# Where eight steps of a dense product stand between five rounds of graph sums

## The chip, the cores and the metric

The kernel runs on one core of one Trainium2 chip. The metric is the device time of one execution in microseconds (us). The core has five engines that run their own queues: TensorE (PE; its weight loads are shown as PEld), VectorE (DVE), ScalarE (ACT), GpSimd (POOL) and SyncE (SP, which here only issues DMAs). Semaphores order them.

## The reference

A pre-norm residual block around a two-layer graph attention network, on 3125 nodes with 768 features and 53125 edges (25000 in each direction and a loop for each node), sorted by destination. A second loop for each node is added inside (in the sum as "2 x"). Layer 1 has 4 heads of 256, layer 2 one head of 768.

```python
def gat_conv(x, edge_index, W, a_src, a_dst, bias, heads, out_ch, concat):
    ...
    xl = (x @ W).reshape(n, heads, out_ch)
    e = leaky_relu(alpha_src[src] + alpha_dst[dst], 0.2)
    m = segment_max(e, dst); e = exp(e - m[dst])
    s = segment_sum(e, dst)
    out = segment_sum(xl[src] * (e / (s[dst] + 1e-16))[:, :, None], dst)
    return out + bias
...
h0 = relu(layernorm(x))
h1 = relu(layer_norm(gat_conv(h0, ..., W1, ...), g1, be1)) + (h0 @ Wr1 + br1)
h  = layer_norm(gat_conv(h1, ..., W2, ...), g2, be2) + (h1 @ Wr2 + br2)
return x + h
```

What matters below is the last but one line: for each node, layer 2 needs a weighted sum over the gathered rows of its neighbours (the graph part), a softmax for its weights, and the dense product h1 @ Wr2 (the residual part).

## The kernel before

The nodes are split into 25 tiles (NB) of 128, the last with 53. First the norm and layer 1 run, then the dense product of layer 2, which writes a table in DRAM: for each node 768 features, its source score and padding, 784 float32. Then follows the loop over the node tiles of layer 2 (from L1232), in which alone the change lies.

*The gathers.* The edges of a tile fill at most 17 slots (J) of 128 edges. `fetch` (L1336) issues one indirect DMA on POOL's queue for each slot (`gather`, L206 to L214): 128 rows of the table into one of 36 buffers (RING). A gather waits until the sums have read what stood in its buffer; so POOL runs two tiles ahead of the sums and no further.

*The sums.* `summed` (L1399) does a tile in five rounds of three or four slots, ROUNDS = (0,5,9,13), (1,6,10,14), (4,11,15), (2,8,16), (3,7,12). They are called r0 to r4 here. A round is 12 to 16 matmuls (L1419): weights are a 128x32 block of the attention weights w, four column quarters of PE run at once, and the 768 features go in two halves of 384 into the PSUM buffer pa. After each round `fetch` asks for as many further slots as the round set free.

*The residual steps.* `residuals` (L1300) is a generator. For each tile it computes h1 @ Wr2 over NK2 = 8 chunks of the contraction; each step, s0 to s7, is one chunk: two dense products (L190), which are four matmuls of 128x384 in the trace. All eight add into one PSUM buffer pr, of which there is one only. s1 also asks SP for the h1 of the tile after next (`load_h1`, L1274), s3 asks SP for the rows of x of the next tile (`load_xr`, L227), and s7 is followed by two sums on DVE (L1315 adds the biases in pr; L1316 adds pr to the rows of x), after which pr is free. `filled(n)` (L1326) runs the next n steps. Three tiles' steps (AHEAD) are run ahead of the loop, so tile b runs the steps of tile b + 3, and the last three tiles have none.

*The softmax of the next tile.* After r2 of tile b, PE transposes the scores of tile b + 1 (L1376, five times 128x128; they were copied from the gathered rows by ACT, L1358), DVE adds the mask and finds the maximum (L1380 to L1385), ACT takes the exponential (L1384, L1387, L1388) and prepares the mask after that (L1363, L1364). After r4, PE transposes the exponentials back (L1392), and DVE and ACT copy them to w (L1395, L1396).

*The end of a tile.* `finish` starts behind r4 (L1432, adds the tile's own rows) and goes on in r0 and r1 of the next tile: L1434, the norm (L514 to L524), L1437, L1438 and the store.

The queues of PE, ACT and DVE run in the order in which the program is written (`tc.manual_schedule`, L1463); those of SP and POOL are ordered by the planner. The list STEPS (L1235) says how many steps `filled` runs behind each round, at the end of the round's turn (L1514). With STEPS = [0, 1, 1, 2, 4] a tile's order on PE is

r0, r1, s0, r2, L1376, s1, r3, s2, s3, r4, L1392, s4, s5, s6, s7.

Of the kernel before, what the change touches and what calls it, by code (L numbers as in the profile page):

```python
# [43 lines left out]
@with_exitstack  # L44
def preln_gat2_kernel(
    ctx: ExitStack,
    tc: tile.TileContext,
    x, src, dst,
    W1, a_src1, a_dst1, b1, g1, be1, Wr1, br1,
    W2, a_src2, a_dst2, b2, g2, be2, Wr2, br2,  # L50
    out,
):

    pool = ctx.enter_context(tc.tile_pool(name="flag", bufs=1))
    flag = pool.tile([1, 1], I32, name="flag")  # L60
    in_order(tc, x, src, dst, W1, a_src1, a_dst1, b1, g1, be1, Wr1, br1,
             W2, a_src2, a_dst2, b2, g2, be2, Wr2, br2, out, flag)
    other = tc.nc.values_load(flag[0:1, 0:1], min_val=0, max_val=1)
    with tc.If(other > 0):
        any_order(tc, x, src, dst, W1, a_src1, a_dst1, b1, g1, be1, Wr1, br1,
                  W2, a_src2, a_dst2, b2, g2, be2, Wr2, br2, out)
# [3 lines left out]
def in_order(  # L70
# [1161 lines left out]
    with tc.tile_pool(name="m2", bufs=1, reuse_waits="tile") as mp, \  # L1232
            tc.tile_pool(name="pg2", bufs=1, space=PSUM, reuse_waits="tile") as pp:
        AHEAD = 3
        STEPS = [0, 1, 1, 2, 4]  # L1235
        RING = 36
        f = C2 // 2

# [87 lines left out]
        def filled(n):  # L1326
            for _ in range(n):
                next(fill, None)
# [128 lines left out]
        def own_share(b):  # L1457
            r = rows_of(b)
            own, v = owns[b][:r], shares[b][1][:r]
            nc.gpsimd.tensor_scalar(own, own, v[:, 2:3], v[:, 3:4], op0=OP.mult, op1=OP.mult)  # L1460
            nc.gpsimd.tensor_tensor(own, own, b2_b[:r], OP.add)

        with tc.manual_schedule(engines={PE, ACT, DVE}):  # L1463
# [16 lines left out]
            for b in range(NB):  # L1480
# [3 lines left out]
                for k in range(len(ROUNDS)):  # L1484
# [23 lines left out]
                    if b + 1 < NB and k == (1 if last else 4):  # L1508
# [3 lines left out]
                        if last:  # L1512
                            own_share(b + 1)
                    filled(STEPS[k])  # L1514
                if b + 2 < NB:
# [476 lines left out]
```

## Time and profile before

| | us |
|---|---|
| median of three runs | 1879.6 |
| their range | 1866.58 to 1886.49 |
| the profiled execution | 1891.63 |
| its span in the trace | 1889.8 |

The span has four stages: up to 1120 the norm and layer 1, to 1264.8 the dense product of layer 2, to 1821.3 the loop over tiles with residual steps, to 1889.8 the last tiles, which have none. By stage (span and its length, then the busy time and number of instructions of PE, PEld, DVE, ACT and POOL, then the clock that PE was granted as a share of full speed, the busy share of the DMA engines and GB/s):

```profile
0.00:1120.00 1120.00, 1083.61 (x7871) 665.12 (x7872) 697.43 (x1963) 224.91 (x604) 445.08 (x463) 0.99 0.78 285
1120.00:1264.80 144.80, 116.61 (x721) 61.57 (x721) 60.36 (x178) 27.12 (x72) 73.13 (x80) 0.95 0.85 316
1821.30:1889.80 68.50, 41.89 (x371) 16.22 (x370) 37.65 (x71) 19.62 (x59) 22.85 (x23) 0.81 0.52 174
```

In the rows of the trace "L190 MATMUL pr<-wr,h" is a group of instructions of line 190 with the tile that is written, the tiles that are read, the shapes and, behind the x, how many there are. A figure in brackets is the idle time of the engine just ahead and what released it; "issue" means that the trace shows nothing for which the engine waited. In a table of waits the columns are the engine and its line, what it waited for, the us in total, how often, and the longest. PE's matmuls overlap, so a group's length is from its first start to its last end.

### The profile page before, as it was taken

Reading aid. Unit: us, or ns where it says so; the run is one execution under the profiler, and the core shown is the slowest. Engines: PE = TensorE matmul, PEld = TensorE weight load, DVE = VectorE, ACT = ScalarE, POOL = GpSimd, SP = SyncE. Lnnn points to the kernel's source line nnn. Section 1 sums busy time; section 2 is a strip of 40 time slices with the busy share of each in tenths; the row PEclk is TensorE's granted clock in tenths of the full one; section 3 lists DMA queues with packets and bytes.
Section 4 is the critical chain, followed back from the end, with each engine's and each line's share of the span. In section 5 each row is a group of like instructions: output and inputs, shape, how many; then the busy total and the mean of one; then the engine's idle time right before and its main releaser. Section 6 shows DMA issues by size and latency. Waiting matters only on the chain.

```text
span 1889.8 us, 31224 instructions
## 1 busy us (share of the span) xinstructions
PE 1718.8 (91%) x11522; PEld 955.7 (51%) x11522; DVE 1006.8 (53%) x2604; ACT 450.9 (24%) x1312; POOL 867.9 (46%) x908
## 2 busy tenths in 40 slices
PE   8999999999899999999999999958888888898885
PEld 5666665666465565555555544423333333343332
DVE  7683436988735665565565566313344343334336
ACT  2222331001211222122122111213333233323332
POOL 2000112000456666666666666255656556555562
PEclk9999999999999999999999999978998998989887
DMA  7833548331799999999999999588989999899883
GB/s 234 291 101 128 139 116 313 125 129 58 263 375 389 374 397 378 405 371 404 345 397 379 360 393 353 205 332 292 318 300 320 326 314 314 293 309 326 303 282 121
DMA packets 172393, 546.67 MB, mean 289 GB/s; under 512 B 30259, under 2 KB 55625, under 8 KB 172104
## 3 DMA queue, kind: packets, MB, share of 16 engines
q0 software_dynamic: 99632, 386.94, 56.5%
q1 hardware_dynamic: 68206, 147.26, 22.6%
q10 hardware_dynamic: 4394, 10.39, 1.4%
q8 instruction: 94, 1.54, 0.3%
q14 instruction: 67, 0.55, 0.1%
HBM read 492.19 MB, written 65.62 MB: 295 GB/s over the span
## 4 chain that ended last, share of the span: by engine, by line
PE 75%; issue 11%; DVE 7%; another core or an unknown queue 2%; DMA 2%; ACT 2%; POOL 0%; SPq 0%; ACTq 0%; DVEq 0%; POOLq 0%
PE pr L190 16%; PE pm L190 11%; PE p L190 11%; PE pa L775 10%; PE pa L1419 10%; PE pm L1027 7%; PE pq L580 3%; PE mix L1392 1%; PE p L1190 1%; DMA w<-in_L_gnn_W_dram 1%; PE mix L1376 1%; DMA g<-table,idx_s 1%; DVE w L752 1%; PE pt L859 1%
## 5 line engine op out<-in xcount | busy, mean ns | idle before, releaser
L210 POOL DMA_INDIRECT g<-table,idx_s x393 | 377.4, 960 | 470.9 <-PE pq L610 167.9
L214 POOL DMA_INDIRECT g<-table,hi_s x423 | 431.5, 1020 | 233.7 <-issue 96.0
L1419 PE MATMUL pa<-g,w 128*32 128x384 f32 x1956 | 230.0, 529 | 77.5 <-issue 63.9
L190 PE MATMUL pr<-wr,h 128*128 128x384 f32 x768 | 285.9, 520 | 3.9 <-issue 3.9
L775 PE MATMUL pa<-g,w 128*32 128x256 f32 x3912 | 261.2, 387 | 14.2 <-issue 7.7
L190 PE MATMUL p<-w,h1T 128*128 128x384 f32 (+1 forms) x768 | 267.7, 496 | 0.2
L190 PEld LDWEIGHTS pr<-wr,h 128*128 128x128 f32 x768 | 150.2, 205 | 121.8 <-issue 50.9
L775 PEld LDWEIGHTS pa<-g,w 128*32 128x32 f32 x3912 | 124.9, 110 | 142.6 <-issue 56.7
L190 PEld LDWEIGHTS p<-w,h1T 128*128 128x128 f32 x768 | 139.8, 189 | 113.2 <-issue 22.2
L1419 PEld LDWEIGHTS pa<-g,w 128*32 128x32 f32 x1956 | 63.4, 114 | 217.1 <-issue 201.9
L752 DVE TENSOR_TENSOR w<-oh,al 128x128 f32<-128x128 f32 (+1 forms) x416 | 131.8, 317 | 60.3 <-PE pa L775 13.9
L190 PE MATMUL pr<-h0k,wr 128*128 128x256 f32 (+1 forms) x576 | 143.9, 393 | 3.6 <-issue 3.1
L1027 PE MATMUL pm<-h0g,wr 128*128 128x512 f32 x288 | 131.9, 605 | 0.0
L190 PE MATMUL pm<-w,h0g 128*128 128x344 f32 x432 | 130.7, 457 | 0.3 <-ACT h0g L861 0.3
L190 PE MATMUL pm<-w,h0l 128*128 128x344 f32 x432 | 129.5, 454 | 0.0
L190 PEld LDWEIGHTS pr<-h0k,wr 128*128 128x128 f32 x576 | 106.0, 191 | 35.9 <-issue 17.0
L751 DVE TENSOR_SCALAR oh<-iota_f,rel_s 128x32 f32<-128x32 f32 (+1 forms) x416 | 113.5, 273 | 1.2 <-issue 0.9
L958 POOL DMA_DIRECT2D hot_d<-ohd x25 | 13.4, 534 | 212.6 <-DVE own L531 128.0
L190 PEld LDWEIGHTS pm<-w,h0g 128*128 128x128 f32 x432 | 81.1, 192 | 39.7 <-issue 0.9
L190 PEld LDWEIGHTS pm<-w,h0l 128*128 128x128 f32 x432 | 80.5, 190 | 39.1 <-issue 0.2
L520 ACT ACTIVATE bn_sd<-bn_mv,eps 128x1 f32<-128x1 f32 (+1 forms) x50 | 14.7, 295 | 353.2 <-DVE bn_mv L516 314.6
L1315 DVE TENSOR_TENSOR pr<-pr,ball_b 128x768 f32<-128x768 f32 x24 | 23.2, 967 | 132.5 <-PE pr L190 62.6
(295 smaller groups left out, 1748.3 us busy)
## 6 DMA issues: line engine op xcount, KB each, us to landing
s<-slo_d SPq DMA_DIRECT2D x25, 544.0 KB
table<-row SPq DMA_DIRECT2D x24, 512.0 KB
own<-table SPq DMA_DIRECT2D x24, 512.0 KB
h1T_d<-h1T SPq DMA_DIRECT2D x24, 512.0 KB
h<-h1T_d SPq DMA_DIRECT2D x22, 512.0 KB
table<-row SPq DMA_DIRECT2D x24, 392.0 KB
ring<-in_x_dram SPq DMA_DIRECT2D x24, 384.0 KB
xr<-in_x_dram SPq DMA_DIRECT2D x24, 384.0 KB
```

The lines of the kernel that those rows point to most:

```text
L190: nc.tensor.matmul(out_, lhsT, rhs, start=start, stop=stop)
L210: nc.gpsimd.indirect_dma_start(out=g, out_offset=None, in_=table[:, :], in_offset=bass.IndirectOffsetOnAxis(ap=idx_s[:, c], axis=0))
L214: nc.gpsimd.indirect_dma_start(out=g, out_offset=None, in_=table[:, :], in_offset=bass.IndirectOffsetOnAxis(ap=idx_k[:, c], axis=0), bound ...
L580: nc.tensor.matmul(q[:, j], oh[:P, o:o + 128], tabs[:, i], start=(i == 0), stop=(i == 2))
L751: nc.vector.tensor_scalar(oh, iota_f[:, lo:hi], rel_s[:, c:c + 1], None, op0=OP.is_equal)
L752: nc.vector.tensor_tensor(w, oh[:, None, :].to_broadcast([128, heads, hi - lo]), al[:, POS[j], :, b:b + 1].to_broadcast([128, heads, hi - ...
L775: nc.tensor.matmul(pa[p0:p0 + 32, o // f, o % f:o % f + n], w[:, o // cols, :], g[:, o:o + n], start=to not in opened, stop=False, skip_gr ...
L859: nc.tensor.transpose(pt[:, k, :r], xt[:, (k0 + k) * 128:(k0 + k + 1) * 128], ident[:r, :r])
L1027: nc.tensor.matmul(pm, wr1[:, k, m * 128:(m + 1) * 128], groups[gi][:, k, :], start=(k == 0), stop=(k == NK1 - 1))
L1190: nc.tensor.transpose(pt[:, k, :r], z[:, (k0 + k) * 128:(k0 + k + 1) * 128], ident[:r, :r])
L1315: nc.vector.tensor_add(pm[:, :, :f], pm[:, :, :f], halves(ball_b))
L1419: nc.tensor.matmul(pa[p0:p0 + 32, i, :f], w_, g[:, i * f:(i + 1) * f], start=(i, q) not in opened, stop=False, skip_group_check=True)
```

## The change

The list of steps behind the five rounds is changed, and nothing else:

```diff
@@ -1232,7 +1232,7 @@
         AHEAD = 3
-        STEPS = [0, 1, 1, 2, 4]
+        STEPS = [1, 1, 1, 1, 4]
         RING = 36
```

The order on PE becomes

r0, s0, r1, s1, r2, L1376, s2, r3, s3, r4, L1392, s4, s5, s6, s7.

s0 now stands between r0 and r1, s1 between r1 and r2, and s2 ahead of r3 with nothing but s3 behind r3. s1's request for h1 moves with it. s3 to s7, their requests and the two sums on DVE stand where they stood.

## The prediction

> **What bounds the kernel now.** I read the busy times by stage first, to see what the changed loop is worth, then the PE timeline of one whole node tile, then POOL's, DVE's and ACT's timelines of the same tile, and last the sums of waits in the loop.
>
> ```profile
> span 1889.8 us, 31224 instructions
> core 0: us, PE busy (x) PEld busy (x) DVE busy (x) ACT busy (x) POOL busy (x), PEclk, DMA share, GB/s
> 1264.80:1821.30 556.50, 476.65 (x2564) 212.79 (x2565) 211.36 (x392) 179.26 (x577) 326.88 (x343) 0.90 0.90 306
> ```
>
> The changed list is used only between 1264.8 and 1821.3 us. PE is busy for 476.65 of 556.5 us there; DVE, ACT and POOL for less than 60% each. In front of and behind this stretch nothing is edited. One tile of it, as PE saw it (start, us, what ran, idle before it):
>
> ```profile
> 1522.88 5.33 PE L190 MATMUL pr<-wr,h 128*128 128x384 f32 x16
> 1528.13 2.79 PE L1419 MATMUL pa<-g,w 128*32 128x384 f32 x32
> 1530.85 1.56 PE L190 MATMUL pr<-wr,h 128*128 128x384 f32 x4
> 1532.34 1.50 PE L1419 MATMUL pa<-g,w 128*32 128x384 f32 x16
> 1533.77 0.77 PE L1376 MATMUL mix<-ident,slots 128*128 128x128 f32 x5
> 1534.37 1.46 PE L190 MATMUL pr<-wr,h 128*128 128x384 f32 x4
> 1535.76 1.50 PE L1419 MATMUL pa<-g,w 128*32 128x384 f32 x16
> 1537.18 2.85 PE L190 MATMUL pr<-wr,h 128*128 128x384 f32 x8
> 1539.96 1.17 PE L1419 MATMUL pa<-g,w 128*32 128x384 f32 x8
> 1541.74 0.48 PE L1419 MATMUL pa<-g,w 128*32 128x384 f32 x1 [0.61 <-issue]
> 1542.47 0.50 PE L1419 MATMUL pa<-g,w 128*32 128x384 f32 x1 [0.25 <-issue]
> 1544.59 0.48 PE L1419 MATMUL pa<-g,w 128*32 128x384 f32 x1 [1.62 <-issue]
> 1545.99 0.95 PE L1419 MATMUL pa<-g,w 128*32 128x384 f32 x5 [0.92 <-issue]
> 1546.87 1.33 PE L1392 MATMUL mix<-ident,e 128*128 128x128 f32 x5
> 1547.99 6.34 PE L190 MATMUL pr<-wr,h 128*128 128x384 f32 x16
> ```
>
> From s4 of one tile to s4 of the next (1522.88 to 1547.99) it is 25.1 us. L1419 are the sums: r0 and r1 run together (32 matmuls from 1528.13), then come step s0 of the residual (L190, 4 matmuls), r2, the score transposes L1376, s1, r3, s2 and s3, r4, the transposes of the exponentials L1392, and s4 to s7. PE runs without a pause up to the middle of r4. There, from 1541.13 (1539.96 + 1.17) to 1545.99, it does three matmuls, and the idle time has no releaser but "issue". What ends this hole stands in POOL's timeline, the gathers for a later tile:
>
> ```profile
> 1517.49 0.95 POOL L210 DMA_INDIRECT g<-table,idx_s  x1 [0.30 <-issue]
> 1519.75 2.20 PE L1419 MATMUL pa<-g,w 128*32 128x384 f32 x5 [0.93 <-issue]
> 1530.36 0.95 POOL L210 DMA_INDIRECT g<-table,idx_s  x1 [3.17 <-PE pa L1419]
> 1535.38 0.95 POOL L210 DMA_INDIRECT g<-table,idx_s  x1 [0.30 <-issue]
> 1540.38 0.95 POOL L210 DMA_INDIRECT g<-table,idx_s  x1 [0.30 <-issue]
> 1542.88 1.00 POOL L214 DMA_INDIRECT g<-table,hi_s  x1 [0.30 <-issue]
> 1546.77 0.94 POOL L210 DMA_INDIRECT g<-table,idx_s  x1 [2.88 <-PE pa L1419]
> 1539.01 0.83 DVE L1380 CUSTOM_DVE_ANT_0 mix<-mix,pen 128x640 f32<-128x640 f32 x1 [6.57 <-remote]
> ```
>
> POOL starts at 1530.36, some 0.8 us after r0's last sum, and issues 11 gathers back to back, one per 1.25 us, until 1543.88. The first four take buffers freed by r0, the next four (from 1535.38) by r1, the last three (from 1540.38) by r2. PE resumes 2.1 us after that run's end; in the tile before, the run ended at 1518.44 and PE resumed 1.3 us later, at 1519.75. While the run lasts, PE's results reach the others late: L1376 ends at 1534.54 by PE's record, but L1380, which needs only that, starts at 1539.01, 4.5 us later. So I read this loop as a cycle: r0 done, POOL's run, 2 us, the rest of r4, L1392, s4 to s7, next r0. PE's own work between r0 and r4 has slack against it.
>
> [...]
>
> **The change part by part.** s0, s1 and s2 each move one round earlier; s3 to s7 stay, with the load of xr that s3 issues and the two DVE sums of s7. Eight steps a tile remain, so PE's total work is the same. The new order is r0 s0 r1 s1 r2 L1376 s2 r3 s3 r4 L1392 s4 to s7, in 22 tiles (25 less the three whose successors' residuals are done ahead).
>
> ```profile
> 1528.24 0.97 DVE L1315 TENSOR_TENSOR pr<-pr,ball_b 128x768 f32<-128x768 f32 x1 [3.96 <-issue]
> 1529.24 0.96 DVE L1316 TENSOR_TENSOR xr<-pr,xr 128x768 f32<-128x768 f32 x1
> 1541.95 0.83 ACT L1387 ACTIVATE e<-e,top 128x640 f32<-128x640 f32 x1
> 1528.23 0.32 SPq L1274 DMA_DIRECT2D h<-h1T_d  x1
> 1543.56 0.33 SPq L227 DMA_DIRECT2D xr<-in_x_dram  x1
> ```
>
> *s0 gets a wait.* It writes the one buffer pr, which L1316 still reads until 1530.20 (1529.24 + 0.96). r0 takes half of 2.79 us and ends at 1529.5. So s0 waits 0.7 us; until now r1's 1.4 us covered that. Everything on PE's queue behind s0 waits with it.
>
> *r1 and r2 finish later.* r1 stands behind the wait and s0's 1.5 us: it ends at about 1533.1, not 1530.9 (+2.2). r2 stands behind s1 as well: 1536.0, not 1533.8 (+2.2). r1's buffers are wanted by POOL at 1535.38 (slack 2.3 left), r2's at 1540.38 (4.4 left by the records).
>
> *The softmax of the next tile starts later.* L1376 ends 2.2 later; with the same lateness L1380 starts at 1541.2, and the exponential L1387, which ends 3.8 us behind L1380's start (1542.78), ends at 1545.0. L1392 takes it at 1546.87, so 4.1 us of cover shrink to 1.9. If it is gone, each further us is one on the path.
>
> *r3 and r4.* r3 ends 2.2 us later, at 1539.5, and POOL wants its buffers at 1546.77. r4 starts only the 0.7 us of s0's wait later, as the same four steps stand ahead of it in both.
>
> *Queues.* s1's load of h1 sits on SP and waits for the previous residual's end anyway (issued at 1528.23, just behind s7's end); s1 itself comes 1.2 us earlier but reads another buffer, loaded a tile before. The xr load (1543.56) stays behind s3. POOL's instructions keep their order. DVE's only edit is that L1380 and the normalization behind it in its queue begin later; L1432 at 1546.98 had 3.44 us of idle before it, so it covers this:
>
> ```profile
> 1546.98 1.02 DVE L1432 SCALAR_TENSOR_TENSOR pa<-own,v,pa 128x768 f32<-128x768 f32 x1 [3.44 <-PE pa L1419]
> PE pa L1419 <- issue: 63.3, 62, 5.9
> ```
>
> *The sum.* What counts is how much of r4 is left when the hole ends. Low end: nothing is lost, because the hole ends with POOL's run, and POOL's run starts with r0, which is not moved: 0. High end: if PE stops after the same number of results, counted from the run's start, then two dense groups (s0 and s1, 8 matmuls) and r1's 16 stand where before r1, s0 and r2 (36) stood, 12 fewer matmuls; 12 sums at 0.09 us (1.50 / 16) are 1.1 us. The 0.7 us of the wait alone would be 0.7. A gain below nothing is the second rival's. Neither end is nearer to a row, since no row shows which matmul PE is held at by count; I take the middle, +0.6 us a tile, times 22: **+13 us**. The profiled execution took 1891.6 us, so it would become 1905. That execution stands 0.6% above the median of the runs shown (1879.6), so on the median I forecast 1879.6 + 13 = **1893 us**.
>
> **The rivals.** *First, slower: r2's results hold up POOL.* The last three gathers need r2's result by about 1539.6 (1540.38 less the 0.8 that r0's took). By the records r2 ends at 1536.0, so this decides once results are more than 3.6 us late; L1376, right behind r2, was 4.5 late. It would cost 0.9 us (4.5 - 3.6) and, if the four extra dense results of s1 come out at the pace of the hole (three matmuls in 4.9 us at the worst; 0.5 us each, my estimate, if L1376's 4.5 us are shared out over its five transposes and r2's last four results), 2 us more: 0.9 to 2.9, say 1.5 us x 22 = +33, 1913 us. For it: the 4.5 us. Against: that is the lateness of L1376, not of r2's own results, which came earlier.
>
> *Second, faster: the run is cut in two.* If POOL has to stop after eight gathers, at about 1540.1, PE's results would come 2.1 us later, at 1542.2, instead of 1546. r4 could end near 1543.5, and L1392 would wait for the exponential: L1380 at 1542.2 plus 3.8 gives 1546.0, 0.9 us sooner than 1546.87. With a shorter hole s4 to s7 run in 5.33 us instead of 6.34, another 1.0:
>
> ```profile
> 1683.29 6.96 PE L190 MATMUL pr<-wr,h 128*128 128x384 f32 x16
> POOL g L210 <- PE pa L1419: 114.1, 39, 8.6
> ```
>
> The same 16 matmuls took 5.33, 6.34 and 6.96 us in three tiles, so up to 1.6 us lie there. Half of the 1.9 us in 22 tiles is -20, all of it -42: 1860 to 1838, and 1860 is what I give it. For it: waits of POOL for sums are cheap now (39 waits, 114.1 us, and the ends of runs are where PE recovers). Against: it needs the very event of the first rival, and then that the later gathers are not missed.
>
> [...]
>
> *Third, nothing happens.* The low end of the sum: POOL's run sets the cycle and all else fits beneath it: 1880 us.
>
> **How the numbers follow.** About 1% (19 us) is what a measurement of this kernel can tell from no change. Forecast (+0 to +1.1 us a tile, 1880 to 1904, middle 1893): chance 0.40; as the top of it and the softmax's thin cover reach over 1%, I put 0.27 of it within 1% and 0.13 slower. First rival 0.22: 0.17 slower, 0.05 within. Second rival 0.23: 0.21 faster, 0.02 within. Third 0.15, all within. Together: faster 0.21, within 1% 0.49, slower 0.30. The range leaves out half of the second rival's chance (below 1860) and the far end of the first's (above 1925, more than 2 us a tile): 1860 to 1925. The forecast's own range is 1880 to 1904.
>
> **What would show it.** Step by step, in a typical tile of the changed kernel: about 0.7 us of PE idle before the first L190 group, released by L1316; r1 and r2 2 us later behind r0; POOL still with a run of 11 gathers 1.25 us apart, first one 0.8 us behind r0 (a run of 8 with a pause in it speaks for a rival, and whether r4 then ends sooner or later says which); the hole in r4 still ending 1.3 to 2.1 us behind that run, with more sums behind it; L1380 about 2 us later, its exponential still ahead of L1392; s4 to s7 still at 5.3 to 7.0 us. The forecast is wrong if L1392 starts to wait for ACT, if POOL pauses within its run, or if the hole is gone.

## The result, and the profile after

| | before | changed |
|---|---|---|
| median, us | 1883.05 (4 runs) | 1939.41 (4 runs) |
| range, us | 1866.58 to 1892.15 | 1928.9 to 1951.44 |
| profiled execution's span, us | 1889.8 | 1927.1 |

The ratio is 1.0306, with a 95% interval of 1.0254 to 1.0358. The changed kernel is slower by 3%, 56 us; the forecast was +13, and the time lies above its range.

First the same stretch of both traces, from the score transposes L1376 of the second tile to those of the twenty-second, 20 tiles (columns as in the table by stage above). Before:

```profile
1273.00:1802.20 529.20, 451.81 (x2444) 202.42 (x2440) 204.67 (x377) 169.49 (x539) 310.66 (x327) 0.91 0.90 309
```

After:

```profile
1274.60:1837.20 562.60, 470.23 (x2441) 197.37 (x2442) 203.44 (x377) 169.49 (x539) 308.41 (x324) 0.92 0.86 289
```

A tile went from 26.5 to 28.1 us (529.2 and 562.6 over 20), which gives 33 of the 37 us between the two spans. (The medians are 56 us apart: the changed kernel's traced execution is the fastest of its four, and that of the kernel before is slower than its median.) The engines run nearly the same number of instructions; the DMA engines are less busy (0.86 after 0.90). So something waits longer. One tile of the changed kernel on PE, with the start of the softmax on DVE in its place by time:

```profile
1535.00 1.50 PE L1419 MATMUL pa<-g,w 128*32 128x384 f32 x16
1537.16 1.53 PE L190 MATMUL pr<-wr,h 128*128 128x384 f32 x4 [0.67 <-PE pa L1419]
1538.62 1.50 PE L1419 MATMUL pa<-g,w 128*32 128x384 f32 x16
...
1541.54 1.50 PE L1419 MATMUL pa<-g,w 128*32 128x384 f32 x16
1542.96 0.77 PE L1376 MATMUL mix<-ident,slots 128*128 128x128 f32 x5
...
1544.95 1.50 PE L1419 MATMUL pa<-g,w 128*32 128x384 f32 x16
...
1547.87 0.83 PE L1419 MATMUL pa<-g,w 128*32 128x384 f32 x2
1549.21 1.18 PE L1419 MATMUL pa<-g,w 128*32 128x384 f32 x3 [0.50 <-issue]
1551.45 0.83 DVE L1380 CUSTOM_DVE_ANT_0 mix<-mix,pen 128x640 f32<-128x640 f32 x1 [12.15 <-remote]
...
1556.98 1.56 PE L1419 MATMUL pa<-g,w 128*32 128x384 f32 x6 [1.62 <-issue]
1558.47 1.33 PE L1392 MATMUL mix<-ident,e 128*128 128x128 f32 x5
1559.60 6.78 PE L190 MATMUL pr<-wr,h 128*128 128x384 f32 x16
```

PE is stopped in r4 as before, but from 1548.7 to 1557.0, 8.3 us in place of 4.9. It does eight matmuls in that time (three in the shown tile of the kernel before), and no single pause is longer than 1.62 us. POOL in the same tile:

```profile
1537.22 0.95 POOL L210 DMA_INDIRECT g<-table,idx_s  x1 [7.66 <-issue]
...
1547.29 0.95 POOL L210 DMA_INDIRECT g<-table,idx_s  x1 [0.30 <-PE pa L1419]
...
1553.56 1.00 POOL L214 DMA_INDIRECT g<-table,hi_s  x1 [0.30 <-issue]
1557.84 0.95 POOL L210 DMA_INDIRECT g<-table,idx_s  x1 [3.27 <-remote]
1559.09 0.95 POOL L210 DMA_INDIRECT g<-table,idx_s  x1 [0.30 <-issue]
1568.53 0.94 POOL L210 DMA_INDIRECT g<-table,idx_s  x1 [8.48 <-issue]
```

The run behind r0 lasts from 1537.22 to 1554.56: 14 gathers 1.25 us apart, where there were 11. PE resumes 2.4 us after its end. The short run behind r4 has 2 gathers in place of 5; then POOL stands idle for 8.5 us until the next r0 is done. Three gathers have moved from the short run into the long one.

The other tiles of the same trace show that r4 grows with the run. From its first start to its last end r4 takes 5.8 to 6.1 us in the tiles with a run of 11 gathers, 7.9 with 12, 9.3 with 13 and 10.6 to 10.7 with 14. (Three of the 20 tiles had broken runs; they took 5.8, 5.2 and 1.5 us. Undisturbed, r4's 16 matmuls take 1.50.)

The three gathers moved in POOL's queue. In the two built programs POOL's instructions are the same, but at 13 tile ends their order differs. Written by the round that sets the gather's buffer free (n0 is the next tile's r0):

```
before   r3 r3 r4 r4 r4 | n0 n0 n0 n0 r1 r1 r1 r1 r2 r2 r2
changed  r3 r3 | n0 r4 r4 r4 n0 n0 n0 r1 r1 r1 r1 r2 r2 r2
```

What stands behind the bar waits until the next tile's r0 is done. The first n0 is the buffer of slot 16. At two of three tile ends the last slot of one tile and the first of the next are one gathered block, so its buffer is free only after the next tile's r0. `fetch` asks for buffers in ring order, so that gather comes ahead of r4's three in the program text. POOL's queue is arranged by the planner; in the kernel before it put r4's three gathers first, in the changed one it does so ever less: 1 of them stands behind n0 at three tile ends, 2 at two and all 3 at eight. The trace bears this out with runs of 12, 13 and 14 gathers at these ends. Why the planner arranged it so is not shown. That is 31 gathers more than before; times 1.25 us 39 us, against 37.3 between the two spans. That these agree so closely is luck, as the medians are 56 us apart.

### The profile page after: what moved, and what is told of

The parts are those of the page before. It is cut to its first block, busy times and chain, and to the rows that moved or that the text cites. A ratio compares the mean times of both kernels' runs of the same rounds, so it can differ in the third digit from the quotient of the medians.

```text
span 1927.1 us, 31193 instructions
## 1 busy us (share of the span) xinstructions
PE 1741.0 (90%) x11522; PEld 951.2 (49%) x11522; DVE 1005.8 (52%) x2604; ACT 451.1 (23%) x1312; POOL 870.4 (45%) x908
## 4 chain that ended last, share of the span: by engine, by line
PE 80%; issue 11%; DVE 4%; another core or an unknown queue 2%; ACT 2%; DMA 1%; SPq 0%; DVEq 0%; ACTq 0%
PE pr L190 17%; PE pm L190 13%; PE p L190 13%; PE pa L775 12%; PE pa L1419 10%; PE pm L1027 7%; PE pq L580 3%; PE p L1190 1%; PE mix L1392 1%; PE pt L859 1%; PE mix L1376 1%; DMA g<-table,hi_s 1%; DVE bn_st L514 0%; DVE xr L1316 0%
## 5 line engine op out<-in xcount | busy, mean ns | idle before, releaser
L1419 PE MATMUL pa<-g,w 128*32 128x384 f32 x1956 | 252.8, 517 | 82.1 <-issue 76.5
L1380 DVE CUSTOM_DVE_ANT_0 mix<-mix,pen 128x640 f32<-128x640 f32 x25 | 20.8, 833 | 259.1 <-remote 251.7
```

The costliest lines, as they stand in the source:

```text
L1380: nc.vector.tensor_tensor_reduce(out=sums_, in0=sums_, in1=pen, scale=1.0, scalar=-BIG, op0=OP.add, op1=OP.max, accum_out=top)
L1419: nc.tensor.matmul(pa[p0:p0 + 32, i, :f], w_, g[:, i * f:(i + 1) * f], start=(i, q) not in opened, stop=False, skip_group_check=True)
```

## The experiments

Theory Q: the time comes from POOL's queue. Theory S: it comes from the moved steps themselves, by s0's wait and the later results of r1 and r2. All times are medians in us; in each comparison the kernels ran beside the kernel before on the same chip. Brackets give the ratio to the kernel before and its 95% interval.

**The changed steps with the queue of before.** `fetch` asks for every buffer that is free, so r4's three come first, and POOL's queue is written out by hand:

```diff
-            while asked < len(slots_due) and asked < min(unused, default=0) + RING:
-                b, j = slots_due[asked]
-                i = asked % RING
+            for a, (b, j) in enumerate(slots_due):
+                if a in asked or (a >= RING and a - RING in unused):
+                    continue
+                i = a % RING
...
-        with tc.manual_schedule(engines={PE, ACT, DVE}):
+        with tc.manual_schedule(engines={PE, ACT, DVE, POOL}):
```

> The changed steps (1, 1, 1, 1, 4), but POOL's queue written out by hand in the order it had before: the three gathers into the buffers of r4 stand ahead of the one that waits for the next tile's r0. Theory Q (the time comes from POOL's queue, where 31 gathers of 1.25 us slid behind a gather that waits for r0, 39 us): within 15 us of the kernel before, about 1885, runs of 11 gathers behind r0. Theory S (the time comes from the steps themselves: s0's wait of 0.7 us and late results of r1 and r2): stays near the changed kernel, 1930 to 1945.

**The old steps with the program's order.** The second half of that diff alone, with `fetch` as it was, so n0 stands first at each of the 14 tile ends that share a block:

> The steps of before (0, 1, 1, 2, 4), but POOL's queue in program order, so that at each of 14 tile ends the gather that waits for the next r0 stands ahead of r4's three. Theory Q: 14 or so times 3 times 1.25 us, some +50 us or more, 1930 to 1945, runs of 14 gathers behind r0 where before there were 11. Theory S: no change, 1875 to 1890.

**The control.** Both halves of the diff, and the old steps:

> The control: the steps of before and POOL's queue written out by hand in the order it had before. Both theories: as before, 1875 to 1890. If the hand-written queue itself costs or gains something, it shows here.

Measured in one comparison, before 1886.98: changed steps with the old queue 1888.62 (ratio 1.0025, 0.9990 to 1.0060); old steps with the program's order 1941.50 (1.0305, 1.0228 to 1.0383); control 1883.90 (0.9978, 0.9941 to 1.0014). One tile of the changed steps with the old queue, the first and the last gather of its run:

```profile
1526.57 0.95 POOL L210 DMA_INDIRECT g<-table,idx_s  x1 [3.90 <-PE pa L1419]
...
1539.10 1.01 POOL L214 DMA_INDIRECT g<-table,hi_s  x1 [0.30 <-issue]
```

and one of the old steps with the program's order, with the end of its r4:

```profile
1547.98 0.95 POOL L210 DMA_INDIRECT g<-table,idx_s  x1 [8.33 <-issue]
...
1564.36 1.01 POOL L214 DMA_INDIRECT g<-table,hi_s  x1 [0.30 <-issue]
1567.06 1.54 PE L1419 MATMUL pa<-g,w 128*32 128x384 f32 x2 [0.61 <-issue]
```

The first run has 11 gathers, the second 14, and 14 stand at each of the 14 shared tile ends of that trace. r4 takes a median of 10.1 us over 20 tiles there, 5.8 with the queue put back, 6.4 in the control and 6.6 in the kernel before.

With the queue put back the loss is gone, and with the queue spoilt and no step moved the loss is there. Q holds and S falls: the steps alone cost 4.7 us (1888.62 less 1883.90). That is not clear of noise: the ten runs of each overlap (1880.9 to 1899.74 and 1874.19 to 1892.78). The queue written by hand is not quite the one of before: by the traces no gather of r4 stands behind n0 in it, where in the kernel before 4 do (1 early in the loop, 3 at its last tile). The two programs that give the 4.7 us share it.

**A queue with a break.** If PE is held as long as POOL's run lasts, the run behind r0 should be cut. On top of the control, r2's three gathers are asked for after r3, behind one that needs r3:

```diff
-        def fetch():
+        def fetch(k=None):
...
+            if k == 2:
+                return
+            due = [a for a in range(len(slots_due)) if a not in asked and (a < RING or a - RING not in unused)]
+            if k == 3 and len(due) > 3:
+                due.insert(0, due.pop(3))
...
```

> The steps of before, and POOL's run behind r0 cut in two: behind the eight gathers of r0 and r1 stands one that waits for r3, ahead of r2's three. If PE is held in r4 because its results come out late as long as POOL's run lasts (theory Q's base), POOL stops after 8 gathers, PE's results come about 2 us later, r4 ends before POOL's second run does, and a tile gets 1 to 3 us shorter: 1815 to 1865, with the hole in r4 gone or under 2.5 us. If the hole has another cause, POOL's later gathers only come later: 1880 to 1920.

Measured in the same comparison: 1856.51 (0.9851, 0.9776 to 0.9925), so faster than the kernel before by 0.7 to 2.2%, and 27 us below the control. In that trace PE around r4 (its lines stand 4 further down, so L1423 are the sums and L1396 is L1392):

```profile
1549.56 2.85 PE L190 MATMUL pr<-wr,h 128*128 128x384 f32 x8
1552.34 1.50 PE L1423 MATMUL pa<-g,w 128*32 128x384 f32 x16
1553.77 0.77 PE L1396 MATMUL mix<-ident,e 128*128 128x128 f32 x5
1554.37 5.33 PE L190 MATMUL pr<-wr,h 128*128 128x384 f32 x16
```

r4 runs through without a hole, and s4 to s7 take 5.33 us. Of 20 tiles r4 takes its undisturbed 1.50 us in 15, and 2.7 at most. But the hold has partly moved: in the tile shown, r2 was held instead, from 1536.7 to 1541.4, where POOL's short run had grown into the long one. Over the 20 tiles PE's pauses with releaser "issue" sum to 20.6 us ahead of the sums, after 45.6 in the control, but to 31.5 ahead of the other groups, after 10.1; together they hardly shrank. PE's busy time did, from 449.29 to 430.93 us, at a granted clock of 0.96 after 0.92. So it is shown that the break wins time and that r4's hole goes with the run, not that PE is held less in all.

**One part of the change at a time.** Steps [1, 0, 1, 2, 4] move s0 alone; [0, 2, 1, 1, 4] move s1 and s2 and leave s0. The built programs show 4 gathers behind n0 for the first, as before, and 41 for the second; 35 for the changed kernel. With them went the changed steps with the break:

> Steps 1, 0, 1, 2, 4: of the change only s0's move ahead of r1, so its wait of 0.7 us for pr is there in 22 tiles; s1 and s2 stand as before, and POOL's queue keeps the order of before. Theory Q: the queue is what costs, so no more than the wait's 15 us, most of it hidden in the hole of r4: 1880 to 1900. Theory S (s0's wait and what it delays is the price): well over 1900, half or more of the +57.

> Steps 0, 2, 1, 1, 4: s0 stays behind r1 and so has no wait for pr; s1 and s2 are a round earlier, r1 ends as early as before. In this program's queue on POOL 41 gathers stand behind one that waits for the next r0, where the kernel before has 4 and the changed one 35. Theory Q: 37 more times 1.25 us = +46, 1925 to 1945. Theory S: no wait of s0 and no later r1, so at most r2's delay, 1880 to 1895.

> The changed steps with the hand-written queue on POOL that has a break behind eight gathers. Theory Q: near the old steps with the same queue (1857), plus the few us that the moved steps cost by themselves: 1850 to 1872, so also faster than the kernel before. If the moved steps cost more once the hole no longer covers s0's wait (22 times 0.7): 1872 to 1885.

This comparison met other conditions: the kernel before took 1767.32 in it. Measured: 1770.45 for s0 alone (1.0017, 1.0004 to 1.0030), 1752.93 for s1 and s2 (0.9923, 0.9900 to 0.9946), 1766.05 for the new steps with the break (0.9987, 0.9973 to 1.0001). The second goes against Q as stated: 41 gathers behind n0, and it is faster. So they were run again, with the changed kernel and the program's order beside them:

> The changed kernel as it is, beside the next three. Where the kernel before takes about 1885 (PE's results late while POOL issues): again 1930 to 1945. Where it takes about 1767 (PE's results 0.1 us behind the record): theory Q2 (a gather slid behind r0 costs only where PE is held as long as POOL's run lasts) says no loss, 1750 to 1775; theory Q1 (a slid gather costs 1.25 us everywhere) says 1767 + 39 = 1806.

> Steps 0, 2, 1, 1, 4 again, with 41 gathers behind one that waits for r0 (35 in the changed kernel, 4 before). Where the kernel before takes about 1885: Q says 37 times 1.25 = +46, 1925 to 1945, theory S (the wait of s0 is the price) 1880 to 1895. Where it takes about 1767: as the last time, 1748 to 1760.

> Steps 1, 0, 1, 2, 4 again, with POOL's queue as before. Where the kernel before takes about 1885: Q says 1880 to 1900, S 1910 or more. Where it takes about 1767: as the last time, 1765 to 1775.

> The steps of before with POOL's queue in program order. Where the kernel before takes about 1885: again 1935 to 1950. Where it takes about 1767: Q2 says 1745 to 1775, as the steps 0, 2, 1, 1, 4 with nearly the same queue took 1753; Q1 says over 1800.

This time the kernel before took 1884.58, and all four fell where Q put them, the last a little above: changed 1936.17 (1.0276, 1.0237 to 1.0316), s1 and s2 1934.19 (1.0251, 1.0216 to 1.0287), s0 alone 1883.52 (1.0005, 0.9976 to 1.0033), program's order 1951.18 (1.0348, 1.0311 to 1.0385). Of the change, s0's move costs nothing that can be told from noise here (its interval is -0.2 to +0.3%), and the move of s1 and s2, which by itself delays no r1 and adds no wait, but moves 37 gathers, costs about what the whole change costs. These two steps with the queue of before were not run alone. The trace of s0 alone (1872.26 us, the fastest of its ten runs) is no plain copy of the kernel before: in the second half of its loop POOL's run is broken into shorter ones, and r4 takes 1.50 us in 11 of 20 tiles, yet a tile still takes 25.6 us (512.6 over 20). So r4's hole is not all that costs time there.

A last comparison asked whether the price of the moved gathers hangs on the conditions:

> The changed steps with the break in POOL's queue, again. Where the kernel before takes about 1885: theory Q says near the old steps with the same queue (1857) plus the few us of the moved steps, 1850 to 1872; S says 1872 to 1900. Where it takes about 1767: as the last time, 1760 to 1772.

> The steps of before with the break in POOL's queue, again. Where the kernel before takes about 1885: as the last time, 1850 to 1865. Where it takes about 1767, PE is not held, so the break has nothing to win: 1755 to 1785.

> The changed kernel. Where the kernel before takes about 1885: 1930 to 1945. Where it takes about 1767: Q2 (the slid gathers cost only where PE is held while POOL's run lasts) 1750 to 1775, Q1 (1.25 us for each everywhere) 1806.

It met the other conditions, before 1765.35. Measured: new steps with the break 1764.08 (0.9995, 0.9982 to 1.0009), old steps with the break 1763.33 (0.9982, 0.9970 to 0.9994), the changed kernel 1755.61 (0.9945, 0.9927 to 0.9962). There the change is a gain of half a per cent, and the break wins almost nothing. The changed kernel's trace in that comparison, first its 20 tiles by the same columns as above, then one tile on PE and DVE:

```profile
1244.90:1683.70 438.80, 401.84 (x2442) 180.90 (x2441) 203.04 (x377) 174.44 (x539) 310.33 (x326) 0.97 0.99 371
```

```profile
1394.85 0.77 PE L1376 MATMUL mix<-ident,slots 128*128 128x128 f32 x5
1395.76 0.83 DVE L1380 CUSTOM_DVE_ANT_0 mix<-mix,pen 128x640 f32<-128x640 f32 x1 [4.57 <-PE mix L1376]
...
1395.46 1.46 PE L190 MATMUL pr<-wr,h 128*128 128x384 f32 x4
1396.84 1.50 PE L1419 MATMUL pa<-g,w 128*32 128x384 f32 x16
1398.27 1.56 PE L190 MATMUL pr<-wr,h 128*128 128x384 f32 x4
1399.76 1.50 PE L1419 MATMUL pa<-g,w 128*32 128x384 f32 x16
1401.19 0.76 PE L1392 MATMUL mix<-ident,e 128*128 128x128 f32 x5
1401.79 5.33 PE L190 MATMUL pr<-wr,h 128*128 128x384 f32 x16
```

L1380 starts 0.1 us behind L1376's recorded end (1395.62), as in every one of the 20 tiles; in the first trace of the same kernel it was 7.7 us in the tile shown (1551.45 less 1543.73), which is also the median of its 20. PE is held nowhere in r4. Its waits in the 20 tiles are two, of which the longer is for rows that have not landed:

```profile
PE mix L1376 <- ACT slots L1358: 23.6, 7, 4.2
PE pr L190 <- PE pa L1419: 13.4, 20, 0.7
```

20 tiles take 438.8 us, 21.9 each, with the DMA engines 0.99 busy: there the transfers are the bound, and a long run of gathers holds nobody up.

The new steps with the break met only these conditions, so what they take where the kernel before takes 1885 was not measured. Why the change gains half a per cent where PE is not held is open too.

## Why the prediction was wrong, step by step

*The step that failed* is one sentence of the part on queues: "POOL's instructions keep their order." The edit touches no gather, and the text of `fetch` is the same; but POOL's queue is ordered by the planner and not by the program, and 31 gathers changed places in it. The sum therefore had no term for a longer run; what it left at nothing measured some 52 us (56.4 less the 4.7 of the moved steps). That the sum then hung on this, the prediction itself said: "POOL's run starts with r0, which is not moved". The start was right. The length of the run, 11 gathers, was taken over from the old trace, and it became 12 to 14 at 13 tile ends. None of the three rivals had this either.

*The price of one moved gather* comes out above the 1.25 us of its issue. Per gather: changed kernel 51.7 us (56.4 less the 4.7 of the steps) over 31, 1.67 us; s1 and s2 alone 49.6 over 37, 1.34; program's order 57.6 over 45 against the control, which has none behind n0, 1.28, and 66.6 over 41 against the kernel before, 1.62. In the trace of the changed kernel r4 grows by about 2.0 us for the first moved gather and 1.4 for each further one. What the part beyond 1.25 us is was not tested.

*The cycle* (r0, POOL's run, 2 us, the rest of r4, L1392, s4 to s7) was right where the kernel before takes 1885. With 14 gathers the hole ends 2.4 us behind the run, with 11 it ended 2.1 us behind, and with the run cut it is gone in 15 of 20 tiles. It is no property of the kernel alone, as the comparisons with 1767 and 1765 show.

*The moved steps* did what the working says, at a lower price. s0's wait is 0.67 us (0.7 forecast). The trace puts it down to PE's own sums, but those had ended before it began; L1316 ends at 1537.06, 0.1 us ahead of s0's start, so the reason given in the prediction fits. r2 ends 8.0 us behind r0's start (1543.04 less 1535.00), 5.7 before: +2.3 (2.2 forecast). For the steps alone +13 was forecast; 4.7 was measured against the control (against the kernel before the interval is -2 to +11 us, 0.9990 to 1.0060 of 1887). The trace of the new steps with the old queue shows, in one tile, where it was tighter than forecast:

```profile
1532.32 0.77 PE L1376 MATMUL mix<-ident,slots 128*128 128x128 f32 x5
1540.89 0.83 DVE L1380 CUSTOM_DVE_ANT_0 mix<-mix,pen 128x640 f32<-128x640 f32 x1 [12.24 <-remote]
1542.19 0.89 PE L1419 MATMUL pa<-g,w 128*32 128x384 f32 x7 [0.63 <-issue]
1544.81 1.19 PE L1392 MATMUL mix<-ident,e 128*128 128x128 f32 x5 [1.73 <-ACT e L1387]
```

I kept L1380's lateness at 4.5 us (over 20 tiles of the kernel before the median was 3.0, so the tile I read was one of its latest); here it is 7.8 (1540.89 less 1533.09). So the cover of 1.9 us that I left to the softmax was gone: L1392 waits 1.73 us for the exponential, once r4 is done. It does so in 10 of 20 tiles, 14.5 us in all, and in 3 tiles of the changed kernel, 5.2 us. That is a second step that failed, though a cheap one: "with the same lateness" did not hold, and the prediction had named L1392's wait as a sign that it was wrong. s1's four matmuls ahead of L1376 are not the reason, as with s1 and s2 alone moved they stand there too and the median is 3.2 us. What makes L1376's results so much later is open.

*First rival (r2's results hold up POOL).* Its direction came true, its mechanism did not. With the queue kept, r2's first gather is the ninth of the run, and it follows the eighth without a pause (1536.60, idle 0.30); in the changed kernel it is the twelfth, as three slid in ahead of it, and it does not wait either (1551.05, idle 0.30). Where the queue is kept, the same late r2 is part of no more than the 4.7 us above. *Second rival (the run is cut in two).* The change doesn't cut it; the break that I put in does, and 1856.51 against the control's 1883.90 is -27 us, between the -20 and -42 given. r4 without a hole fits the mechanism; that part of the hold turned up elsewhere was not in it. That a shorter hole gives s4 to s7 in 5.33 us was my estimate from the lengths in three tiles; the runs agree with it only in part. With the break s4 to s7 took 5.33 us behind an r4 without a hole. They took 6.34 us at a granted clock of 0.84 behind the kernel before's hole of 4.9 us (PE busy for 1.5 us of it), and 6.78 us at 0.78 behind the changed kernel's of 8.3 us (busy for 3.0 us). But s4 to s7 are not slow behind every hole: in the kernel before, those at 1522.88 took 5.33 us at a clock of 1.00 behind a hole of 4.1 us (1515.62 to 1519.75). There the slow clock (0.52 from 1519.75 to 1522.88) fell on the end of r4 and on L1392. What lowers the clock was not tested.

## What to carry to other kernels

When only some queues are written out by hand, compare the built program's other queues before and after any edit, even one that touches none of their instructions: a planner may reorder them. In a queue that runs in order, an instruction that waits for a late event must not stand ahead of ones that could go (here 45 gathers behind such ones cost 57.6 us where the kernel before takes 1887); ask which instruction is first to block, and what stands behind it. And a change whose price is a wait that no row of the trace explains should be timed under more than one condition: this one was +3% in two comparisons and -0.5% in another.

## What the hardware showed that I had not expected

The same program took 1883 to 1887 us in three comparisons and 1765 to 1767 us in two. For four of the five the record names the chip, each time another one: 13 and 7 with 1887 and 1885, 9 and 10 with 1767 and 1765. That fits a difference between chips; but no chip was used twice, so a condition that comes and goes is not excluded. In the first kind, PE's results reach the other engines up to 7.8 us behind PE's recorded ends while POOL issues gathers back to back, PE is stopped in r4, and the DMA engines move 289 GB/s at a busy share of 0.86; in the second kind the results are 0.1 us behind under the same gathers, and the DMA engines move 371 GB/s at 0.99 (the changed kernel in both). Per busy share that is 336 and 375 GB/s, so the transfers are slower in the first kind too. What makes PE's results late there stays open: POOL's issuing and the transfers that it sets off were never parted, though the second kind moves more bytes per us without it.
